# Layer 0, the deformable convolution: a ring of small column tiles in place of two tiles of 18 taps, thirteen gather buffers, twelve combined tiles

## The chip, the cores and the metric

The kernel runs on one core of a Trainium2 chip. The metric is the time of one execution on the device in microseconds (us), taken as the median of several runs. The engines are called as the profile calls them: PE (TensorE, matrix products and transposes; PEld is its weight load), DVE (VectorE), ACT (ScalarE), POOL (GpSimd), SP (SyncE, which only issues transfers here).

## The reference, cut to what matters

A batch of four images (256 channels, 64 by 64 points) goes through four layers, each of the form x = x + layer(groupnorm(x)): a deformable convolution (layer 0), an attention block (layer 1), a grouped deformable operator (layer 2) and a state-space layer (layer 3). Only layer 0 is changed. Cut down, it is:

```python
offset = conv3x3(xn, offset_w) + offset_b             # 18 numbers per point: dy, dx for each of 9 taps
mask = 2 * sigmoid(conv3x3(xn, mod_w) + mod_b)        # 9 numbers per point
for each point p and each of the 9 taps k:
    py, px = p + tap k + offset[k, p]                 # a place between four pixels
    val[:, k, p] = bilinear(xn, py, px) * mask[k, p]  # 4 pixels x 256 channels, weighted
out[o, p] = sum over c, k of weight[o, c, k] * val[c, k, p]
x = x + out
```

So every point needs, for each of nine taps, four pixels of 256 channels from a place that the data decide: 4 KB per point and tap.

## The kernel before, in words

The four images are done one after the other, and layers 0 to 3 one after the other within an image. Layer 0 works from a table in device memory (`tab`) in which one row of 1024 numbers holds the four neighbouring pixels of a place. For the first image the table is built at the start of layer 0; for images 2 to 4 layer 3 of the image before has built it already, with the mean and the deviation (`known`) and the first sixteen sets of points.

The points of an image are 32 tiles of 128 points. A step q is one tap of one tile: 32 x 9 = 288 steps per image. Two tiles go together as a group m, so a group has 18 steps; `where(q)` gives the group, the tile and the tap. Each step passes through these functions, called with a growing lag behind the step number (0, 2, 3, 4, 6, 7):

- `along` (lag 0): POOL issues an indirect transfer (L486) that fetches 128 rows of `tab` into a gather buffer `g` (128 x 1024 numbers, 4 KB per partition, from the pool `pg`). ACT multiplies the left pixels by their weight into a row tile `r` (L496), and DVE adds the weighted right pixels (L497). After L497 the gather buffer is free.
- `across` (lag 2): ACT (L506) and DVE (L507) combine the upper and the lower row into the combined tile `acc` (128 x 256).
- `turn` (lag 3, every second step): PE transposes the two `acc` tiles of one tap into PSUM (L516).
- `copy` (lag 4, every second step): ACT (even taps) or DVE (odd taps) copies the turned columns into `cols` (L523).
- `products` (lag 6): PE multiplies them by the weights `l0w` and sums over the 18 steps of the group in PSUM (L534).
- `add` (lag 7): at a group's end DVE adds the sum to x (L546).

The order on PE, ACT and DVE is written out by hand (`manual_schedule`), so each of them does these steps in the order in which they are called. POOL and SP are not in that list; what they issue is ordered by the scheduler. A buffer's number of copies (`bufs`) says how many steps later its memory may be written again.

In images 2 to 4 more lies beside this at the start. POOL issues the load of the offset weights (`l`, L138). DVE clears the borders of the normalised image `xnp` (L455) and fills 49 rows of it with 14 instructions (L458), ahead of its first L497. PE does the remaining offset convolutions (`offsets`, L372) between the steps, listed in `after`; a part of them follows each of the first 18 steps and every third step after that. They read `xnp` and `l`.

Of the kernel before, what the change touches and what calls it, by code (L numbers as in the profile page):

```python
# [9 lines left out]
F32 = mybir.dt.float32  # L10
# [6 lines left out]
P = 128  # L17
# [46 lines left out]
class Net:  # L64
# [270 lines left out]
    def layer0(self, x, weights):  # L335


        nc, tc = self.nc, self.tc
        tab, known, self.known = self.tab, self.known, None
        with (  # L340
# [2 lines left out]
            tc.tile_pool(name="l0d", bufs=2) as pd,  # L343
            tc.tile_pool(name="l0x", bufs=1) as px,
            tc.tile_pool(name="l0r", bufs=5) as pr,
            tc.tile_pool(name="l0g", bufs=9) as pg,
            ExitStack() as start,
        ):
            self.psum = start.enter_context(self.banks(8))
# [84 lines left out]
            with (  # L434
# [7 lines left out]
                rows, accs, cols, turned, sums = {}, {}, {}, {}, {}  # L442
# [34 lines left out]
                def where(q):  # L477

                    m, r = q // (2 * K2), q % (2 * K2)
                    return m, 2 * m + r % 2, r // 2  # L480
# [18 lines left out]
                def across(q):  # L499

                    _, t, k = where(q)
                    a = accs[q] = pd.tile([P, 256], F32, tag="acc", name="acc", bufs=6)
                    r = rows.pop(q)
                    wy = spots[t // 8][2]
                    t = t % 8
                    nc.scalar.mul(a, r[:, 0, :], wy[:, 0, t, k : k + 1])  # L506
                    nc.vector.scalar_tensor_tensor(a, r[:, 1, :], wy[:, 1, t, k : k + 1], a, ALU.mult, ALU.add)  # L507
# [10 lines left out]
                def copy(q):  # L518
                    if q % 2:
                        m, _, k = where(q)  # L520
                        if k == 0:
                            cols[m] = pd.tile([P, 18, 256], F32, tag="cols", name="cols")
                        (nc.vector.tensor_copy if k % 2 else nc.scalar.copy)(  # L523
                            cols[m][:, 2 * k : 2 * k + 2, :].rearrange("p i c -> p (i c)"), turned.pop(q)
                        )

                def products(q):

                    m, t, k = where(q)
                    i = 2 * k + t % 2  # L530
                    if i == 0:
                        sums[m] = psum2.tile([P, 2, 512], F32, tag="pz", name="pz")
                    for ot in range(2):
                        nc.tensor.matmul(  # L534
                            sums[m][:, ot, :256],
                            wf[:, i, bass.ts(ot, P)],
                            cols[m][:, i, :],
                            start=(i == 0),
                            stop=(i == 17),
                        )  # L540
# [10 lines left out]
                for q in range(steps + 8):  # L551
                    for lag, do in ((0, along), (2, across), (3, turn), (4, copy), (6, products), (7, add)):
                        if 0 <= q - lag < steps:
                            do(q - lag)
                    for do in after.get(q, ()):
                        do()
# [1526 lines left out]
```

## Time and profile before

| | |
|---|---|
| median of 3 runs | 8875.99 us (8872.48 to 8886.61) |
| the profiled execution: its time, its span | 8856.17 us, 8854.4 us |
| busy share of the span: PE, DVE, POOL, ACT | 91%, 88%, 78%, 56% |
| granted PE clock, mean | 0.971 of full speed |
| gather stage, image 1: first L486 to the end of the last L546 | 96.1 to 570.3, 474.2 us |
| image 2 | 2271.7 to 2764.7, 493.0 us |
| image 3 | 4465.3 to 4950.6, 485.3 us |
| image 4 | 6649.5 to 7137.3, 487.8 us |

The four gather stages together take 1940.3 us, 22% of the span. The profile's lines name the source line, the engine, the operation, the tile written and the tile read. An arrow in brackets names what ended the idle time ahead of an instruction; "issue" is idle time without a visible cause, and "remote" is the profile's name for another core or a queue that it does not know.

### The profile page before, as it was taken

The page shows a single profiled execution, that of the slowest core. Times are in us where ns is not written, and L with a number is a line of the kernel's source. Part 1 is how long each engine was busy: PE and PEld are TensorE (multiplying, and loading weights), DVE is VectorE, ACT ScalarE, POOL GpSimd, SP SyncE. Part 2 cuts the span into 40 slices and gives each one's busy share as a digit, 9 for nine tenths or more (in the row PEclk, how much of TensorE's full clock was granted, in tenths as well). Part 3 has the DMA queues.
Part 4 walks back from the last instruction along what each step waited for, and adds up shares of the span by engine and source line. Part 5 has one row for each costly group of instructions (what it writes and reads, how often), then busy time and mean ns, then how long its engine had stood idle before and what let it go on. Part 6 is the DMA issues. An engine that isn't in the chain of part 4 may idle for free.

```text
span 8854.4 us, 96956 instructions
## 1 busy us (share of the span) xinstructions
PE 8048.8 (91%) x31063; PEld 4243.5 (48%) x31063; DVE 7769.1 (88%) x9912; ACT 5001.6 (56%) x7642; POOL 6905.6 (78%) x4407
## 2 busy tenths in 40 slices
PE   6789998998878999899888899989988799989997
PEld 4653474443564347344356435634435643564443
DVE  6788798999888879899988788899998788889998
ACT  4753436666674343666667434376666743446664
POOL 4757797999674779799967477889996747789997
PEclk8999999999999999999999999999999999999999
DMA  8950112445884012244588301123458810122343
GB/s 301 330 180 10 36 57 62 111 114 148 296 321 146 10 41 62 66 113 114 160 308 320 111 10 46 60 81 111 111 171 321 317 68 1 48 63 78 107 107 80
DMA packets 457946, 1149.71 MB, mean 130 GB/s; under 512 B 51425, under 2 KB 119018, under 8 KB 446160
## 3 DMA queue, kind: packets, MB, share of 16 engines
q0 software_dynamic: 178800, 681.04, 23.2%
q1 hardware_dynamic: 278624, 462.37, 16.9%
q8 instruction: 248, 4.06, 0.2%
q14 instruction: 274, 2.24, 0.1%
HBM read 905.84 MB, written 88.10 MB: 112 GB/s over the span
## 4 chain that ended last, share of the span: by engine, by line
DVE 36%; PE 31%; POOL 9%; issue 9%; ACT 6%; DMA 5%; SPq 2%; another core or an unknown queue 1%; DVEq 0%; POOLq 0%; ACTq 0%
DVE h L1906 19%; PE cx L712 11%; DVE h L1815 7%; DMA g<-tab,idx 4%; PE sc L682 3%; POOL h L1930 3%; PE pm L592 3%; DVE r L497 2%; PE pz L534 2%; PE pacc L1036 2%; SPq L889 2%; DVE acc L507 2%; POOL g L486 2%; PE y L1774 2%; ACT r L496 2%
## 5 line engine op out<-in xcount | busy, mean ns | idle before, releaser
L1930 POOL TENSOR_TENSOR h<-h,cn 128x2048 f32<-128x2048 f32 x508 | 2300.5, 4528 | 41.5 <-POOL carry L1927 0.2
L1906 DVE TENSOR_TENSOR_SCAN h<-da,carry,h 128x512 f32<-128x512 f32 x1636 | 1984.6, 1266 | 73.2 <-ACT da L1904 25.1
L1904 ACT ACTIVATE da<-delta,l3a 128x512 f32<-128x512 f32 x2048 | 1392.1, 689 | 1040.5 <-DVE h L1906 1036.3
L1774 PE MATMUL y<-h,ident 128*128 128x512 f32 x4096 | 1908.3, 599 | 4.0 <-POOL h L1930 4.0
L486 POOL DMA_INDIRECT g<-tab,idx x1152 | 1320.2, 1146 | 565.3 <-DVE r L497 269.4
L706 POOL TENSOR_TENSOR acc<-acc,e 128x1024 f32<-128x1024 f32 x472 | 1110.0, 2352 | 353.0 <-ACT e L697 333.9
L534 PE MATMUL pz<-cols,l0w 128*128 128x256 f32 x4608 | 1211.5, 407 | 136.3 <-issue 64.4
L1774 PEld LDWEIGHTS y<-h,ident 128*128 128x128 f32 x4096 | 783.0, 193 | 1017.9 <-issue 950.7
L497 DVE SCALAR_TENSOR_TENSOR r<-g,wx,r 128x512 f32<-128x512 f32 x1152 | 860.3, 747 | 329.4 <-ACT r L496 220.2
L697 ACT ACTIVATE e<-e 128x1024 f32<-128x1024 f32 x512 | 541.3, 1057 | 899.7 <-DVE e L696 793.1
L534 PEld LDWEIGHTS pz<-cols,l0w 128*128 128x128 f32 x4608 | 882.1, 203 | 325.3 <-issue 115.8
L712 PE MATMUL cx<-e,v 128*128 128x512 f32 x2048 | 1002.2, 615 | 2.3 <-ACT e L697 2.3
L496 ACT ACTIVATE r<-g,wx 128x512 f32<-128x512 f32 x1152 | 825.7, 717 | 210.8 <-DMA g<-tab,idx 169.7
L1815 DVE TENSOR_TENSOR h<-du,bn 128x1536 f32<-128x1536 f32 (+1 forms) x512 | 938.5, 1833 | 4.6 <-PE bn L1800 4.4
L1011 DVE TENSOR_TENSOR prod<-ring,A 128x768 f32<-128x768 f32 (+1 forms) x640 | 715.9, 1161 | 48.8 <-DMA ring<-ring 31.5
L696 DVE TENSOR_TENSOR e<-sc,mr 128x512 f32<-128x512 f32 x1024 | 639.1, 682 | 126.0 <-PE sc L682 125.0
L1036 PE MATMUL pacc<-ident,prod 128*128 128x128 f32 x5120 | 664.7, 280 | 47.7 <-POOL prod L1025 18.8
L605 DVE TENSOR_REDUCE m<-pm 128x1 f32<-128x512 f32 x896 | 556.0, 683 | 110.3 <-PE pm L592 110.3
L712 PEld LDWEIGHTS cx<-e,v 128*128 128x128 f32 x2048 | 350.2, 189 | 603.5 <-issue 437.0
L516 PE MATMUL pt<-ident,acc 128*128 128x128 f32 x2304 | 422.4, 292 | 228.1 <-DVE acc L507 179.3
L1036 PEld LDWEIGHTS pacc<-ident,prod 128*128 128x128 f32 x5120 | 564.2, 142 | 136.6 <-POOL prod L1025 50.1
L506 ACT ACTIVATE acc<-r,wy 128x256 f32<-128x256 f32 x1152 | 571.8, 497 | 29.1 <-DVE r L497 24.5
(309 smaller groups left out, 11958.1 us busy)
## 6 DMA issues: line engine op xcount, KB each, us to landing
cn<-cd SPq DMA_DIRECT2D x512, 256.0 KB
bs<-cd SPq DMA_DIRECT2D x412, 256.0 KB
delta<-du POOLq DMA_DIRECT2D x48, 1024.0 KB
tab<-vtnext SPq DMA_DIRECT2D x192, 256.0 KB
ring<-ring SPq DMA_DIRECT2D x288, 126.0 KB
ring<-ring SPq DMA_DIRECT2D x288, 120.0 KB
delta<-w POOLq DMA_DIRECT2D x24, 1024.0 KB
g<-tab,idx POOLq DMA_INDIRECT x1152
```

Of the source, the lines that this page charges most:

```text
L486: nc.gpsimd.indirect_dma_start(out=g[:], out_offset=None, in_=tab[:, :], in_offset=bass.IndirectOffsetOnAxis(ap=spots[t // 8][0][:, t % 8, ...
L496: nc.scalar.mul(r, g[:, :, 0, :], wx[:, 0, t, k : k + 1])
L497: nc.vector.scalar_tensor_tensor(r, g[:, :, 1, :], wx[:, 1, t, k : k + 1], r, ALU.mult, ALU.add)
L534: nc.tensor.matmul(sums[m][:, ot, :256], wf[:, i, bass.ts(ot, P)], cols[m][:, i, :], start=(i == 0), stop=(i == 17),)
L706: nc.gpsimd.tensor_add(b["acc"], b["acc"], e)
L712: nc.tensor.matmul(blocks[qb]["cx"], v[:, 4 * (i + kt // 4 * 4) + kt % 4, :], e[:, bass.ts(i % 2, 512)], start=(kt == 0 and i == 0), stop= ...
L1036: nc.tensor.matmul(d["pd"][:, ct, t, :], prod[:, x, t, bass.ts(ct, P)], self.ident, is_transpose=True, start=(wy == 0 and x == left[0] and ...
L1774: nc.tensor.matmul(c["ys", dc], self.ident, h[:, dc, :], start=False, stop=(n == DS - 1), skip_group_check=(j == 0))
L1815: nc.vector.tensor_mul(h[:, :d, :], c["du"][:, :d, :], c.pop(("bn", n)).to_broadcast([P, d, C]))
L1904: nc.scalar.activation(da, c["delta"][:, dc, :], AF.Exp, scale=al[:, dc, n : n + 1])
L1906: nc.vector.tensor_tensor_scan(h[:, dc, :], da, hb, carry[:, dc, n : n + 1], ALU.mult, ALU.add)
L1930: nc.gpsimd.tensor_mul(h, h, cn.to_broadcast([P, 4, C]))
```

## The change

`cols` was one tile per group, [128, 18, 256], in two copies: 36,864 bytes per partition. It becomes one tile per tap and pair of point tiles, [128, 2, 256], in six copies: 12,288 bytes. The gather buffers go from nine to thirteen (36,864 to 53,248 bytes), and the combined tiles from six to twelve (6,144 to 12,288 bytes). Layer 0's pools are 2,048 bytes smaller in sum, and several of them lie at other addresses than before. The instructions of PE, ACT and DVE in layer 0 are the same in kind and number.

```diff
-            tc.tile_pool(name="l0g", bufs=9) as pg,
+            tc.tile_pool(name="l0g", bufs=13) as pg,
...
-                    a = accs[q] = pd.tile([P, 256], F32, tag="acc", name="acc", bufs=6)
+                    a = accs[q] = pd.tile([P, 256], F32, tag="acc", name="acc", bufs=12)
...
                     if q % 2:
                         m, _, k = where(q)
-                        if k == 0:
-                            cols[m] = pd.tile([P, 18, 256], F32, tag="cols", name="cols")
+                        c = cols[m, k] = pd.tile([P, 2, 256], F32, tag="cols", name="cols", bufs=6)
                         (nc.vector.tensor_copy if k % 2 else nc.scalar.copy)(
-                            cols[m][:, 2 * k : 2 * k + 2, :].rearrange("p i c -> p (i c)"), turned.pop(q)
+                            c.rearrange("p i c -> p (i c)"), turned.pop(q)
                         )
...
                             wf[:, i, bass.ts(ot, P)],
-                            cols[m][:, i, :],
+                            cols[m, k][:, t % 2, :],
```

## The prediction

> **What bounds the kernel now.** The page first, for the lines of the changed stage:
>
> ```profile
> L486 POOL DMA_INDIRECT g<-tab,idx x1152 | 1320.2, 1146 | 565.3 <-DVE r L497 269.4
> L534 PE MATMUL pz<-cols,l0w 128*128 128x256 f32 x4608 | 1211.5, 407 | 136.3 <-issue 64.4
> L497 DVE SCALAR_TENSOR_TENSOR r<-g,wx,r 128x512 f32<-128x512 f32 x1152 | 860.3, 747 | 329.4 <-ACT r L496 220.2
> L496 ACT ACTIVATE r<-g,wx 128x512 f32<-128x512 f32 x1152 | 825.7, 717 | 210.8 <-DMA g<-tab,idx 169.7
> ```
>
> Everybody waits for everybody: POOL for a free buffer (DVE's L497), ACT for a gather that has not landed, DVE for ACT. So I cut the span into windows: the four gather stages, then a stretch of image 2 with offset convolutions, then two short stretches of image 1.
>
> ```profile
> 96.10:570.30 474.20, 376.01 (x1728) 297.99 (x1728) 378.77 (x691) 345.76 (x656) 339.67 (x288) 0.90 0.89 321
> 2271.70:2764.70 493.00, 408.38 (x2041) 300.50 (x2039) 387.58 (x741) 349.59 (x673) 326.53 (x288) 0.93 0.88 317
> 2305.00:2400.00 95.00, 91.80 (x557) 58.61 (x555) 76.84 (x150) 70.43 (x139) 59.66 (x57) 1.00 0.88 313
> 270.00:285.00 15.00, 14.88 (x79) 12.34 (x78) 14.96 (x29) 14.27 (x29) 12.87 (x8) 1.00 0.77 258
> 355.00:361.00 6.00, 5.44 (x28) 4.16 (x27) 5.42 (x11) 5.69 (x11) 4.78 (x5) 1.00 1.02 407
> ```
>
> The columns are window and length, then busy us of PE, PEld, DVE, ACT, POOL, then clock, DMA share, GB/s. No engine is full over a stage: image 1 has PE 376, DVE 379, POOL 340 of 474 us; the transfers run at 321 GB/s though 407 is seen in 355 to 361. In 2305 to 2400 PE is full (91.8 of 95 us): there the gathers do not set the pace. Elsewhere the stage swings. In 270 to 285 DVE is full and POOL issues only 8 gathers in 15 us; at other times DVE starves. The timeline shows why POOL is slow there:
>
> ```profile
> 280.07 4.33 POOL L486 DMA_INDIRECT g<-tab,idx  x1 [0.30 <-DVE r L497]
> 280.32 0.75 DVE L497 SCALAR_TENSOR_TENSOR r<-g,wx,r 128x512 f32<-128x512 f32 x1
> ...
> 283.11 0.48 DVE L507 SCALAR_TENSOR_TENSOR acc<-r,wy,acc 128x256 f32<-128x256 f32 x1
> 283.50 0.68 DVE L546 TENSOR_TENSOR x<-pz,x 128x512 f32<-128x512 f32 x1
> ```
>
> A gather whose median is 0.94 us takes 4.33 us while L497 and L507 follow each other without a gap, and ends just after L546, which reads PSUM. The other half of the swing:
>
> ```profile
> 306.08 0.93 POOL L486 DMA_INDIRECT g<-tab,idx  x1 [0.31 <-issue]
> 308.09 0.58 ACT L523 COPY cols<-pt 128x512 f32<-128x512 f32 x1 [6.57 <-remote]
> 310.35 0.94 POOL L486 DMA_INDIRECT g<-tab,idx  x1 [3.33 <-DVE r L497]
> ```
>
> ACT stands still for 6.57 us at a copy, for a reason that the profile does not name; POOL goes on until the nine buffers are full and then idles 3.33 us. Image 1 has eight such stops of 3.5 to 6.6 us on ACT or DVE.
>
> **The change, part by part.** The *column ring* saves no instruction. The copy of a tap follows the products of the tap twelve steps before on PE, and before that copy ACT or DVE has waited for a later transpose on PE anyway; in the built program the copies wait for PE alone, as before. Price 0, with no cover needed. *Twelve combined tiles* take PE from the semaphores that L507 waits for in the steady state. The line's own view shows no idle time ahead of L507, since `copy` has already tied DVE to PE. Price 0.
>
> *Thirteen gather buffers* are the change. POOL's timeline gives the gap ahead of each gather; 0.30 us is the usual one. What exceeds it and ends in L497 sums to 28.1, 57.8, 44.4 and 49.2 us in images 1 to 4, 179.5 us in all, longest 4.8 us. Four more buffers hold 4 x (0.94 + 0.30) = 4.96 us of issuing, so they cover even the longest of these waits. In images 2 to 4 I leave out the first 130 us, where PE sets the pace: 37.8 + 31.4 + 27.9, with image 1's 27.9 after its first 25 us, makes 125.0 us, or 125.0 / 1.24 = 101 gathers that are issued earlier.
>
> What is one of them worth? In a full stretch such as 270 to 285 POOL delivers 8/15 = 0.533 gathers per us, and DVE takes 1/1.315 = 0.760 steps per us (378.8 us of DVE work over 288 steps). A spare gather then lengthens the stretch by 1/(0.760 - 0.533) = 4.4 us, in which 3.3 steps go at 1.315 us, not at the stage's mean of 1.64: 1.1 us gained. So 101 gathers are worth at most 111 us. The other side agrees: after each stage's first 25 us ACT waits for gathers at L496 for 39.2, 24.6, 25.3 and 27.7 us, 116.8 us together.
>
> I take half of 111, 56 us. What is late next stands close behind: in the same stages ACT's copy waits for PE's transposes (21.5, 44.7, 21.2, 25.4 us), PE is busy 405 to 408 of 485 to 493 us in images 2 to 4, and the unnamed stops stay. The bounds for this term are 0 (a spare gather is eaten up by a slower POOL) and 111. The built program sets a second limit: each gather waits for the landing of the gather eight before it, so thirteen buffers never mean more than eight transfers in flight. POOL's waits for a landing are 26.1 us in 49 waits now; they may grow, at most by what the buffer waits lose.
>
> The rule that speaks against the change is in the Trainium skill, SBUF — State Buffer, section "SBUF: two separate sides": DVE and GpSimd share a port pair as an exclusive lock, and a DVE instruction with two SBUF inputs blocks a GpSimd one that reads SBUF. The 4.33 us gather above fits it (L497 and L507 read two SBUF tiles, a gather its indices); if the rule held without any gap, every us of DVE work gained would block POOL as long, and the sum would be 0, not 56.
>
> *The moved addresses.* At the start of images 2 to 4 the built program differs. Five gathers now stand ahead of the load of `l` on POOL; that load, and DVE's first L455, wait for the last L1606 matmul of layer 3 (before, neither did). The trace of image 2:
>
> ```profile
> 2270.81 0.60 POOL L138 DMA_DIRECT2D l<-in_l  x1 [7.87 <-DVE sres L1875]
> 2271.71 1.04 POOL L486 DMA_INDIRECT g<-tab,idx  x1 [0.30 <-issue]
> 2273.73 6.04 DVE L458 TENSOR_SCALAR xnp<-x,gm,rs 128x64 f32<-128x64 f32 x14
> 2275.02 3.60 PE L1606 MATMUL out<-sres,l3b 128*128 128x512 f32 x8
> 2286.70 0.75 DVE L497 SCALAR_TENSOR_TENSOR r<-g,wx,r 128x512 f32<-128x512 f32 x1 [2.71 <-ACT r L496]
> 2291.29 0.75 DVE L497 SCALAR_TENSOR_TENSOR r<-g,wx,r 128x512 f32<-128x512 f32 x1 [3.44 <-ACT r L496]
> ```
>
> L1606 ends at 2278.6. Gathers 1 to 5 go out 0.9 us earlier, `l` 7.9 us later, and POOL stands some 2 us at it with the sixth gather and all later ones behind. L455 starts at 2278.6 in place of 2272.7, 5.9 us later, and all of ACT's and PE's steps wait behind DVE's first L497 (2279.7, then about 2285.5). Cover: before, DVE's fourth and fifth L497 waited 2.71 and 3.44 us for gathers, so with five gathers landed it has caught up by about 2291. PE's first L372 waits for `l` and `xnp`, some 5 us later, and PE idles 9.2 us between 2281 and 2295 now, waiting for DVE's L507. I price this at +1 us per image, +3 in all; with no cover 3 x 5.9 = +18; if the earlier gathers win, -3.
>
> Sum: 56 - 3 = 53 us. The profiled execution's 8856.2 becomes 8803; it lies 19.8 us below the median of the runs, so the median goes from 8876.0 to **8823**.
>
> **The rivals.** *All starvation goes*: the 111 us term in full, 8876 - 111 + 3 = 8768. For it: the buffers cover every wait, and DVE's 379 us plus the 40 us of image 1's eight stops leave the 474 us stage 55 us of room. Against: PE's waits come next. Chance 0.15.
>
> *No change*: the backlog is eaten up. Thirteen buffers keep DVE gapless longer, POOL stays at 15/8 = 1.88 us per gather, and the stage only swings more slowly; 8876 within 18 us. For it: the 8 gathers in 15 us. Against: during a stop (303.6 to 306.1) POOL issues every 1.24 us and then idles only for want of buffers. Chance 0.22.
>
> *Slower*: the later normalisation is not covered. Place: DVE's queue ahead of the first L497 in images 2 to 4. Price 5.9 us each, and when the late `l` pushes PE's offset convolutions into the PE-bound stretch, up to 8 us each: 3 x 8 = 24, so 8900. It decides if gathers 1 to 5 have landed well before 2285 and PE has no idle time left before the full stretch; and only if the buffers bring nothing. Chance 0.15.
>
> That the rings do nothing is part of the forecast, not a rival.
>
> **How the numbers follow.** The forecast (8823; own range 8785 to 8858, a gain of 18 to 91 us) has 0.48. A change below 0.2%, 18 us, is not told from none here. Faster is 0.48 + 0.15 = 0.63, the same 0.22, slower 0.15. The range 8748 to 8892 reaches past the first rival and most of the way to the last, and leaves out about 0.05 below and 0.13 above.
>
> **What would show it.** POOL's waits for L497 in the gather stages fall from 269 us to below 160 (0.30 each is the floor), ACT's waits for gathers at L496 from 170 to 100 to 130, the stages to 455 to 475 us; L507 and the copies wait as before. Gathers above 1.5 us (22 in image 1, 15 in each other) become more, not fewer: if their excess grows by as much as the waits fall, the second rival is right. In images 2 to 4 DVE's first L497 comes 6 us later after the first gather. The forecast is wrong if the stages keep their length though POOL waits less, or if the unnamed stops grow.

## The result, and the profile after

The change makes the kernel slower: 8932.08 us (median of 6 runs, 8916.75 to 8945.43) against 8881.30 us for the kernel before beside it (8863.04 to 8897.61). The ratio is 1.0052, with a 95% interval of 1.0038 to 1.0065. The forecast was 8823 us with a range of 8748 to 8892: the direction was wrong, and the range did not hold it.

The later sets of runs, each with the kernel before beside it, fall into two conditions: the kernel before takes either about 8890 us (called A here, and so it was for the prediction and the result) or about 8715 us (B), the whole set long and whatever the kernel, and one chip gave both. Every ratio below is taken within one set.

The profiled execution of after has a span of 8915.0 us, 60.6 us more than before's 8854.4. The four gather stages take 500.1, 491.1, 492.8 and 511.1 us, together 1995.1 against 1940.3: 54.8 of the 60.6 us lie there. From line 522 on, line numbers are one lower than before.

The page of after, for the same groups as before (busy us and mean ns of one | idle time before them, and what ended most of it):

```profile
L486 POOL DMA_INDIRECT g<-tab,idx x1152 | 1387.5, 1204 | 560.7 <-issue 232.5
L533 PE MATMUL pz<-cols,l0w 128*128 128x256 f32 x4608 | 1204.3, 406 | 165.2 <-issue 77.7
L497 DVE SCALAR_TENSOR_TENSOR r<-g,wx,r 128x512 f32<-128x512 f32 x1152 | 859.6, 747 | 286.3 <-ACT r L496 140.9
...
L496 ACT ACTIVATE r<-g,wx 128x512 f32<-128x512 f32 x1152 | 825.8, 717 | 165.3 <-DMA g<-tab,idx 140.2
```

POOL's waits for a buffer are no longer the largest cause of its idle time, and ACT waits less for gathers: 140.2 us against 169.7. That is the direction that was forecast, and yet the stages are longer. POOL's mean gather went from 1146 to 1204 ns. The windows of the stages of images 1, 2 and 4 (length, busy us of PE, PEld, DVE, ACT, POOL, clock, DMA share, GB/s):

```profile
96.90:597.00 500.10, 376.83 (x1728) 298.10 (x1728) 377.17 (x692) 342.98 (x656) 362.50 (x288) 0.89 0.85 305
2301.00:2792.00 491.00, 402.71 (x2042) 297.43 (x2040) 387.71 (x742) 347.59 (x673) 344.37 (x289) 0.93 0.89 318
6683.40:7194.40 511.00, 408.40 (x2042) 298.73 (x2040) 387.69 (x742) 349.16 (x673) 338.99 (x289) 0.93 0.85 305
```

PE, DVE and ACT do the same work as before in more time, and the transfers run slower over the stage (305 GB/s in image 1 against 321). The time went into standstills. The list of waits names who waits for whom (sum, count, longest). First before, then after:

```profile
ACT cols L523 <- remote: 135.1, 30, 7.6
...
DVE cols L523 <- remote: 20.1, 9, 4.3
```

```profile
POOL g L486 <- DVE r L497: 232.3, 266, 6.0
...
ACT cols L522 <- remote: 146.0, 28, 13.5
...
DVE cols L522 <- remote: 69.9, 16, 10.8
...
DVE x L545 <- remote: 39.7, 6, 8.2
```

POOL's waits for L497 fell by 37 us only (from 269.4). The stops that the profile puts down to "remote" became longer: 13.5 us at most in place of 7.6. Two of them, one on DVE and one on ACT, in the timeline of after (start, duration, engine, line):

```profile
6933.92 0.72 PE L516 MATMUL pt<-ident,acc 128*128 128x128 f32 x4
...
6934.47 1.89 PE L533 MATMUL pz<-cols,l0w 128*128 128x256 f32 x8
...
6936.20 0.82 PE L516 MATMUL pt<-ident,acc 128*128 128x128 f32 x4
...
6937.83 0.94 POOL L486 DMA_INDIRECT g<-tab,idx  x1 [0.30 <-issue]
...
6944.10 0.95 POOL L486 DMA_INDIRECT g<-tab,idx  x1 [0.30 <-issue]
6944.66 0.69 DVE L522 COPY cols<-pt 128x512 f32<-128x512 f32 x1 [8.13 <-remote]
...
6945.41 3.73 PE L533 MATMUL pz<-cols,l0w 128*128 128x256 f32 x8 [8.38 <-issue]
...
6948.97 0.60 PE L516 MATMUL pt<-ident,acc 128*128 128x128 f32 x4
...
6951.78 0.59 ACT L522 COPY cols<-pt 128x512 f32<-128x512 f32 x1 [13.49 <-remote]
```

The n-th copy of an image needs the n-th four transposes. Those that DVE's copy at 6944.66 needs are the four at 6933.92, which end at 6934.64 by the modelled end. The trace also records updates of the semaphore by which PE tells that it is done: the one for these transposes comes at 6944.64, 10.0 us after the modelled end and 0.02 us before the copy. So "remote" is PE, told late. ACT's copy at 6951.78 needs the four transposes at 6936.20, which end at 6937.03; their update comes at 6951.76. By then PE has run the eight products at 6945.41 and the four transposes at 6948.97, which stand behind them in its order. So what is late is the signal, not PE's work. ACT's semaphore in the same stretch is on time (6938.31, for an L506 that ends at 6938.30). Until 6944.66 POOL issues a gather every 1.25 us; DVE and ACT stand, since their order is fixed and the copy stands ahead of their next blends.

This holds in general. Of the 576 copies in after's gather stages 44 wait longer than 3 us, 265.7 us together, and in 42 of these the copy starts within 0.1 us of an update of PE's semaphore; the transposes that these copies need had ended, by their modelled ends, a median 6.1 and at most 14.8 us earlier. Before has 35 such waits with 168.7 us and a longest of 7.6.

### The profile page after: what moved, and what is told of

The parts are those of the page before. It is cut to its first block, busy times and chain, and to the rows that moved or that the text cites. A ratio compares the mean times of both kernels' runs of the same rounds, so it can differ in the third digit from the quotient of the medians.

```text
span 8915.0 us, 96880 instructions
## 1 busy us (share of the span) xinstructions
PE 8056.2 (90%) x31063; PEld 4247.0 (48%) x31063; DVE 7765.8 (87%) x9912; ACT 4995.7 (56%) x7642; POOL 6976.1 (78%) x4407
## 4 chain that ended last, share of the span: by engine, by line
DVE 37%; PE 29%; POOL 10%; issue 10%; DMA 6%; ACT 5%; SPq 2%; another core or an unknown queue 1%; DVEq 0%; POOLq 0%; ACTq 0%
DVE h L1905 19%; PE cx L711 10%; DVE h L1814 7%; DMA g<-tab,idx 5%; PE sc L681 3%; POOL h L1929 3%; PE pm L591 3%; DVE r L497 3%; POOL g L486 3%; PE pacc L1035 2%; SPq L888 2%; DVE acc L507 2%; PE y L1773 2%; ACT r L496 1%; DVE prod L1010 1%
## 5 line engine op out<-in xcount | busy, mean ns | idle before, releaser
L486 POOL DMA_INDIRECT g<-tab,idx x1152 | 1387.5, 1204 | 560.7 <-issue 232.5
L497 DVE SCALAR_TENSOR_TENSOR r<-g,wx,r 128x512 f32<-128x512 f32 x1152 | 859.6, 747 | 286.3 <-ACT r L496 140.9
L496 ACT ACTIVATE r<-g,wx 128x512 f32<-128x512 f32 x1152 | 825.8, 717 | 165.3 <-DMA g<-tab,idx 140.2
L506 ACT ACTIVATE acc<-r,wy 128x256 f32<-128x256 f32 x1152 | 573.3, 498 | 80.4 <-DVE r L497 54.3
```

The costliest lines, as they stand in the source:

```text
L486: nc.gpsimd.indirect_dma_start(out=g[:], out_offset=None, in_=tab[:, :], in_offset=bass.IndirectOffsetOnAxis(ap=spots[t // 8][0][:, t % 8, ...
L496: nc.scalar.mul(r, g[:, :, 0, :], wx[:, 0, t, k : k + 1])
L497: nc.vector.scalar_tensor_tensor(r, g[:, :, 1, :], wx[:, 1, t, k : k + 1], r, ALU.mult, ALU.add)
```

## The experiments

### Set one, condition A: how many buffers, and which part

```diff
# e1_nine, e1_eleven, e1_seven: after, with
-            tc.tile_pool(name="l0g", bufs=13) as pg,
+            tc.tile_pool(name="l0g", bufs=9) as pg,      # 11, 7
# e1_acc_six: after, with
-  ... name="acc", bufs=12)
+  ... name="acc", bufs=6)
```

> The changed kernel with the gather buffers put back to nine; the ring of turned columns and the twelve combined tiles stay. Theory A (a stop at the copies and adds lasts as long as GpSimd can go on issuing gathers, so more buffers make longer stops): within 0.2% of the kernel before (8881 us beside it), stages of layer 0 that sum to 1930 to 1950 us instead of 1995, and no idle time above 8 us ahead of a copy or an add. Theory B (the ring of columns or the twelve combined tiles are what costs): as slow as the changed kernel, 40 to 55 us above before, stages near 1995. Theory C (the moved addresses at the starts of images 2 to 4): first blend (L497) 15 us after the first gather in images 2 to 4 as in the changed kernel, and 15 to 25 us above before, if the addresses of this version still collide.

> The changed kernel with eleven gather buffers. Theory A: between the two, 20 to 30 us above the kernel before, longest stops 8 to 11 us (two more gathers of 1.25 us than with nine). Theory B: as slow as with thirteen, 40 to 55 us above before. The port theory (the vector engine without pauses blocks GpSimd) expects the gathers' durations above 0.94 us to sum between 238 (before) and 305 (changed).

> The changed kernel with seven gather buffers. Theory A: stops of at most 5 to 6 us, but GpSimd waits for a buffer more often (over 400 us of waits for L497 instead of 269 before); if the stops were the whole cost, 20 to 40 us faster than before; if the earlier accounting of the buffers' worth (1.1 us a gather) holds, 20 to 60 us slower than before. Theory B: as slow as the changed kernel or slower still.

> The changed kernel with six combined tiles instead of twelve; thirteen gather buffers and the ring stay. Theory A: same as the changed kernel within 0.2%, 40 to 55 us above before. If the twelve tiles were the cost, at most 20 us above before.

Measured against 8885.79 us for the kernel before. Waits and gathers are those of the gather stages in one profile each. The row of the kernel before is the profile that the prediction read, that of after, with its ratio, is from the result, and the second row of the kernel before is a profile from set four:

| kernel | ratio (95%) | copies waiting over 3 us: number, sum, longest | gathers' time above 0.94 us | span of the profile |
|---|---|---|---|---|
| seven buffers | 0.9970 (0.9961 to 0.9979) | 34, 132 us, 5.0 us | 191 us | 8846.9 |
| kernel before (nine) | 1 | 35, 169 us, 7.6 us | 239 us | 8854.4 |
| kernel before (nine), set four | 1 | 53, 242 us, 7.8 us | 258 us | 8901.7 |
| nine | 0.9999 (0.9990 to 1.0009) | 48, 230 us, 7.7 us | 239 us | 8891.7 |
| eleven | 1.0049 (1.0035 to 1.0063) | 45, 268 us, 10.9 us | 273 us | 8915.0 |
| thirteen (after) | 1.0052 (1.0038 to 1.0065) | 44, 266 us, 13.5 us | 305 us | 8915.0 |
| thirteen, six combined tiles | 1.0067 (1.0053 to 1.0081) | 45, 308 us, 13.5 us | 287 us | 8924.7 |

The ring of columns and the twelve combined tiles cost nothing: with nine buffers the changed kernel is level with before, and with six combined tiles it is no faster. The buffers are the cost, and fewer of them than before are a gain. That ends theories B and C: in the version with nine, L497 starts 14.5 to 14.8 us after the first gather in images 2 to 4, against 8.0 before, and costs nothing that can be seen. Two expectations missed: with nine buffers the stages sum to 1973 us in place of 1930 to 1950, in a profile that lies 10.8 us above that version's median, and with seven POOL waits 299 us for L497, not over 400.

The longest wait follows the number of buffers. The lists of waits with seven, with nine and with eleven:

```profile
ACT cols L522 <- remote: 101.6, 38, 5.0
```

```profile
ACT cols L522 <- remote: 159.6, 35, 7.7
```

```profile
ACT cols L522 <- remote: 191.5, 33, 10.9
```

From seven to thirteen it grows by 8.5 us in six buffers, 1.4 us each, close to the 1.25 us that POOL needs per gather. This is what theory A says. The sum of these waits differs much between two profiles of the same kernel (169 and 242 us for the kernel before), so one profile's sum does not measure the buffers; but the spans go with the sums, 78 us of span for 176 us of waits from the first row to the last. The buffers set how long a stop can get: in the longest wait of the versions with seven, nine, eleven and thirteen, POOL issued 3, 5, 7 and 9 gathers between the modelled end of the transposes and the copy, and had then stood idle for 1.2 to 2.6 us. Not every stop lasts until POOL has no free buffer left, as theory A has it in full: DVE's above ends while POOL still issues.

### Sets two and three, condition B: no stops, no effect

Set two (kernel before 8712.38 us) and set three (8715.98 us) ran on two other chips.

```diff
# e2_seven_columns_old: before, with bufs=7 for l0g
# e3_thirteen: after; e3_seven: as e1_seven
# e2_seven_later, e2_thirteen_later, e3_thirteen_later: after with 7 or 13 buffers, and
-  for q in range(steps + 8):
-      for lag, do in (..., (4, copy), (6, products), (7, add)):
+  for q in range(steps + 10):
+      for lag, do in (..., (6, copy), (8, products), (9, add)):
# e2_quarter_bytes, e3_quarter_bytes: after, with
-  out=g[:], ... in_=tab[:, :],
+  out=g[:, :256], ... in_=tab.rearrange("r (s c) -> (r s) c", c=256),
-  g = g.rearrange("p (y x c) -> p y x c", y=2, x=2)
+  g = g[:, None, None, :256].to_broadcast([P, 2, 2, 256])
```

> The kernel before with one edit: seven gather buffers instead of nine, its two big column tiles and six combined tiles kept. Theory A (a stop lasts as long as gathers can still be issued): 20 to 45 us faster than before, as seven buffers did in the changed kernel (0.997), longest wait for PE ahead of a copy near 5 us instead of 7.6. Theory B (ring of columns or more combined tiles give what seven buffers showed): no faster than before.

> The changed kernel itself once more, for a second chip: the chip of the second set of runs gave 8712 us for the kernel before (the first gave 8886), and its traces show no wait named remote ahead of a copy. Where the kernel before takes about 8880 us: ratio 1.004 to 1.007 again. Where it takes about 8710: if the stops are the whole cost of the change, ratio 0.996 to 1.002, stages that sum to 1770 to 1800 us; if the change costs something besides the stops (the later first blend in images 2 to 4, three times 6.9 us, or GpSimd's longer gathers), ratio 1.002 to 1.005.

> The changed kernel with seven gather buffers once more. Where the kernel before takes about 8880 us: 0.996 to 0.998 as before. Where it takes about 8710: 0.999 to 1.002 (seven buffers with the old columns gave 0.9997 there), with the first blend 14.6 us after the first gather in images 2 to 4 against 8.0 with the old columns.

Seven buffers with the old columns: 0.9997 (0.9988 to 1.0006). After itself: 0.9998 (0.9989 to 1.0007). Seven buffers in after: 0.9997 (0.9988 to 1.0006). In B the number of buffers makes no difference that can be seen, and no copy of the 576 waits longer than 3 us in the profiles of after, with thirteen or with seven buffers. The waits of after in B:

```profile
POOL g L486 <- DVE r L497: 183.9, 436, 2.5
ACT r L496 <- DMA g<-tab,idx: 182.0, 250, 19.6
...
ACT cols L522 <- PE pt L516: 99.4, 105, 2.7
```

There is no "remote", and every copy that waits starts 0.04 us after the modelled end of its transposes. After's span is 206 us shorter than in A (8709.0 in place of 8915.0), 202 us of it in the four gather stages. Where the stops are missing, the cost of the change is missing too. But the gain that was forecast is missing here too, where no stop can eat it. The windows of image 1 show where it went, with thirteen and then with seven buffers:

```profile
96.30:528.60 432.30, 357.64 (x1728) 278.68 (x1728) 380.81 (x691) 350.59 (x656) 330.73 (x288) 0.97 0.95 352
```

```profile
96.70:525.40 428.70, 362.36 (x1728) 284.83 (x1728) 380.31 (x691) 350.52 (x656) 315.53 (x288) 0.94 0.95 355
```

With thirteen POOL is busy 15.2 us longer for the same 288 gathers. Gap by gap it waits 1.3 us in the whole stage beyond the usual 0.30 us per gather, against 13.4 us with seven; its gathers' time above 0.94 us is 60.2 us against 44.9. The two add up to 61.5 and 58.3 us: each us of waiting that the buffers saved came back as longer gathers. POOL then runs from end to end, 288 x 1.24 + 61.5 = 419 us plus the last steps. In images 2 to 4 the gathers of a stage, from the first to the last, take 79.0 to 86.3 us beyond 288 x 1.24 in both versions, the load of `l` among them.

> The changed kernel with thirteen buffers, in which each gathered row is 1 KB instead of 4 KB (the blends read that quarter four times, so the rows and the result are others; 1152 gathers, all instructions and all waits stay). If the saturated transfers (400 GB/s and more during a stop) make the stops: no wait above 4 us ahead of a copy, idle time ahead of copies and adds under 150 us, stages of 440 us or less. If GpSimd's issuing itself makes them: the stops stay as long as with thirteen buffers (up to 10 to 13 us) with 100 GB/s moved.

> Thirteen buffers with 1 KB rows instead of 4 KB (other rows, other result; all instructions and waits stay). Where the kernel before takes about 8880 us and stops are seen: if saturated transfers make them, no wait named remote above 4 us ahead of a copy and 60 to 180 us faster than the changed kernel; if GpSimd's issuing makes them, the stops stay and the time is within 20 us of it. Where it takes about 8710: about 1.003, as the one run there (8745).

Quarter rows: one run of 8744.96 us in set two, 1.0025 (1.0015 to 1.0036) in set three. The window of image 1 in set three:

```profile
96.20:545.80 449.60, 364.04 (x1728) 285.23 (x1728) 381.11 (x691) 350.90 (x656) 351.49 (x288) 0.95 0.29 87
```

The transfers fill 29% of their time in place of 95%, and the stage is not shorter. So bytes are not what holds it in B. POOL again has no waits to speak of (1.4 us beyond the usual gaps), and its gathers take 80.8 us above 0.94. On the stops this says nothing, since B has none.

> The changed kernel with seven gather buffers and the copies two steps later (lag 6 instead of 4, products 8, adds 9), so that ACT and DVE reach a copy some 2.6 us later than PE's transposes allow. If the stops are late signals from PE of a length that the buffers set (longest 5.0 us with seven), two steps cover more than half of each: waits for PE ahead of copies fall from 236 us (ACT) to under 120 us, stages sum to 1850 to 1890 us instead of 1931, 40 to 80 us faster than seven buffers alone. If the pause of PE, ACT and DVE is one common standstill, whatever they wait for, the waits only move to other lines and the time stays within 0.2% of seven buffers alone (8853 us).

> The changed kernel with the copies two steps later and thirteen gather buffers as in the change. If the signals are late by a length that the buffers set: the longest waits of 13.5 us shrink to about 11 us and those under 3 us vanish, 50 to 90 us faster than the changed kernel. If it is a common standstill: within 0.2% of the changed kernel (8930 us).

> Thirteen buffers with the copies two steps later. Where the kernel before takes about 8880 us and stops are seen: if the stops are late signals from PE, waits ahead of copies named remote fall from 216 us (ACT and DVE together) to under 120 and the time is 20 to 60 us below the changed kernel; if they are a common standstill, within 0.2% of it. Where it takes about 8710: 1.001 again.

Later copies: 1.0018 (1.0009 to 1.0027) with seven buffers, 1.0012 (1.0003 to 1.0021) with thirteen in both sets. With thirteen, in set three:

```profile
ACT r L496 <- DMA g<-tab,idx: 230.4, 328, 20.2
...
POOL g L486 <- DVE r L497: 118.0, 374, 1.0
...
ACT cols L522 <- PE pt L516: 14.7, 11, 2.5
```

ACT's waits for PE's transposes fall from 99.4 to 14.7 us, and its waits for gathers rise from 182.0 to 230.4. What is taken off one wait goes to the gathers, and their mean goes to 1195 ns from 1143. That fits a stage that goes at POOL's own pace in B. It is not shown: the run that would show it, with the gathers freed from DVE in B, was not made.

### Set four, condition A: the gathers freed from the vector engine

```diff
# e4_fixed_psum: after, with one PSUM bank of zeros as second input of both blends
-  nc.vector.scalar_tensor_tensor(r, g[:, :, 1, :], wx[...], r, ALU.mult, ALU.add)
+  nc.vector.scalar_tensor_tensor(r, g[:, :, 1, :], wx[...], zero, ALU.mult, ALU.add)
-  nc.vector.scalar_tensor_tensor(a, r[:, 1, :], wy[...], a, ALU.mult, ALU.add)
+  nc.vector.scalar_tensor_tensor(a, r[:, 1, :], wy[...], zero[:, 0, :], ALU.mult, ALU.add)
# e4_psum_blend (thirteen buffers), e4_psum_blend_nine: ACT writes its half of r to PSUM
-  nc.scalar.mul(r, g[:, :, 0, :], wx[...])
-  nc.vector.scalar_tensor_tensor(r, g[:, :, 1, :], wx[...], r, ALU.mult, ALU.add)
+  h = psum3.tile([P, 2, 256], F32, tag="ph", name="ph")      # two banks
+  nc.scalar.mul(h, g[:, :, 0, :], wx[...])
+  nc.vector.scalar_tensor_tensor(r, g[:, :, 1, :], wx[...], h, ALU.mult, ALU.add)
# in all three: pz is [P, 2, 256] in one bank, with one start and one stop for both sums
```

> The changed kernel with thirteen buffers, in which both blends of the vector engine (L497, L507) take a constant PSUM bank of zeros as second input instead of what ACT wrote to SBUF: each has one SBUF input and one PSUM input, and the first halves of the sums are left out (result differs); to free a bank the two sums of pz lie in one bank. All instructions, buffers and nearly all waits stay. Port theory (GpSimd's gather is blocked while a vector instruction with two SBUF inputs runs): gathers all near 0.94 us, excess over 0.94 us under 60 us in all instead of 234 to 305, GpSimd no longer wall to wall, stages of 400 to 430 us, 80 to 200 us faster than the kernel before. Rival (the transfers or ACT's chain bound the stage): excess may fall but stages stay within 10 us of 432 to 454 (chip without stops).

> The changed kernel with thirteen buffers, in which ACT writes the first half of the blend across x (L496) to a PSUM bank of two, and the vector engine's L497 reads it there and writes r to SBUF; the sums are complete. L507 keeps its two SBUF inputs. Port theory: the part of L497 (860 of 1410 us of such instructions) goes, gathers' excess falls by about 60%, 30 to 120 us faster than the kernel before. Rival: within 0.2% of it, or slower if reading PSUM makes L497 longer than 0.75 us (each 0.05 us is 58 us) or two banks are too few for ACT to run ahead.

> The same with nine gather buffers. Port theory with GpSimd free: buffers decide even less; on a chip without stops within 0.2% of the version with thirteen; on one with stops 30 to 50 us faster than that.

> The kernel before itself, for a trace on this chip. If the chip has no stops (8710 us): no wait named remote ahead of a copy, L486's waits for a buffer 220 to 240 us in all, gathers' excess near 200 us, stages that sum to 1775 to 1795 us.

The set came out in A: the kernel before at 8898.84 us. A line of its page, then its waits:

```profile
L486 POOL DMA_INDIRECT g<-tab,idx x1152 | 1340.6, 1164 | 571.6 <-DVE r L497 271.0
```

```profile
ACT r L496 <- DMA g<-tab,idx: 156.1, 143, 20.3
...
ACT cols L523 <- remote: 147.9, 40, 7.8
ACT cols L523 <- PE pt L516: 141.2, 118, 7.5
```

The same two of the version with zeros in PSUM:

```profile
L489 POOL DMA_INDIRECT g<-tab,idx x1152 | 1087.0, 944 | 826.6 <-DVE r L500 463.9
```

```profile
ACT cols L525 <- PE pt L519: 221.5, 136, 7.6
...
ACT cols L525 <- remote: 202.0, 64, 6.4
...
ACT r L499 <- DMA g<-tab,idx: 48.2, 18, 20.2
```

The port theory is right about the gathers. With one SBUF input in DVE's blends the 1152 gathers take 0.94 us in the mean and 1.26 us at most, the excess over 0.94 falls from 258 to 5 us, and DVE's L500 takes as long as L497 (744 against 749 ns). ACT has few waits for gathers left. The 80 to 200 us that the theory expected did not come. The time is 1.0002 (0.9992 to 1.0011) of before, and the stages sum to 1985 us against 1975. ACT's waits for gathers fell by 108 us, and its waits for PE ahead of the copies rose by 134, to 424 us. In A the supply of gathers does not set the stage. What took its place is the wait for PE's late signals: 98 copies wait over 3 us, 378 us together, in place of 53 and 242.

With the real blend through PSUM the ratio is 1.0018 (1.0009 to 1.0027) with thirteen buffers and 1.0005 (0.9996 to 1.0014) with nine, so thirteen buffers are no better than nine here either. L507 keeps its two SBUF inputs in these two versions, and still the excess is only 15 and 11 us, where the expectation left some 40% of it.

### Set five: the same chip as set four, condition B

> Thirteen buffers with 1 KB rows instead of 4 KB (other rows, other result; instructions and waits stay), for a chip where the kernel before takes about 8890 us. If the transfers make PE's signals late: no wait named remote above 4 us ahead of a copy, stages of 450 to 460 us as on the chips without stops, 130 to 170 us faster than the kernel before. If something of the chip other than the transfers makes them late: stages of 480 to 500 us, within 0.5% of the kernel before. Where the kernel before takes about 8710: 1.0025 again, and the question stays open.

> Seven buffers with the copies two steps later, for a chip where the kernel before takes about 8890 us. If late signals of PE are all that stops ACT and DVE: two steps cover 2.6 us of each, waits ahead of copies under 120 us in all instead of 295 (seven buffers), 40 to 80 us faster than seven buffers alone, so ratio 0.988 to 0.993. If PE's own pace is what bounds the stage there: the waits stay or move to the adds and to PE, ratio 0.996 to 1.000. Where the kernel before takes about 8710: 1.002 again.

The kernel before took 8715.01 us on the chip that had given 8898.84. Quarter rows gave 1.0039 (1.0025 to 1.0052), later copies with seven buffers 1.0026 (1.0017 to 1.0035), both as in B before. So the stops are no property of a chip. Whether the transfers make PE late in A, and whether later copies help there, was not measured.

## Why the prediction was wrong, point by point

Two steps failed: the worth of the thirteen buffers, in both conditions, and the price of the stops, in A.

- **"The unnamed stops stay."** This step failed in A. The stops were read, counted (eight in image 1) and priced at nothing, although the lines shown had POOL issuing all through a stop until the nine buffers were full. They are waits for PE's signal, the longest of them grows with the number of buffers, and the 46 to 51 us by which after is slower go with them: the loss is there in A and is 0 in B, where no such wait is. The prediction named their growth as what would refute it.
- **"Half of 111, 56 us" for the thirteen buffers.** This step failed in both conditions, and it was mis-sized: in B, where no stop interferes, it measures 0 (0.9998). A spare gather was priced by the starvation that it ends, with the later gathers' durations left as they were. They grew by as much as the waits fell: waits and growth together are 61.5 us with thirteen buffers and 58.3 with seven, in image 1. The rival "no change: the backlog is eaten up" described what B shows. In A the term is 0 for another reason: even gathers for which ACT hardly waits (48 us in place of 156) do not shorten the stages (1985 against 1975 us).
- **The rule weighed against the change.** The Trainium skill, SBUF — State Buffer, section "SBUF: two separate sides", taken without any gap as the prediction did, would have made the sum 0. The set with zeros in PSUM agrees with the mechanism (1164 to 944 ns per gather once DVE has one SBUF input), and B agrees with the sum. The versions in which L507 alone keeps two SBUF inputs (952 and 948 ns) show much less blocking than the expectation had left for it. Taking half as a compromise was the mistake: the 4.33 us gather was among the lines read.
- **"Price 0" for the ring and the combined tiles.** Right: 0.9999 with nine buffers.
- **"The moved addresses, +3."** The shift came as said (first L497 at 14.7 to 14.9 us in images 2 to 4 in place of 8.0). Its cost stays inside the interval of the nine-buffer ratio, 8 us at most. The rival that built on it, "Slower", had the right sign for the wrong reason: image 1, which has no such start, lost 25.9 us between the two profiles.
- **What would show it.** POOL's waits for L497 at 232 us in place of under 160; ACT's waits for gathers at 140 in place of 100 to 130; stages of 491 to 511 in place of 455 to 475. Gathers above 1.5 us did become more: 27, 19, 21 and 18 against 22, 15, 15 and 15.

What stays open is why PE reports late in A. What is shown is when. In after, the transfers run at 369 to 415 GB/s during every such wait of over 5 us; in the fastest twentieth of image 2's stage they reach 414 and more. But in B they run above 395 GB/s more often (32% of 2 us slices of after's image 2, against 19% in A) without one late signal, so full transfers alone are not the cause. In A the trace also holds fewer updates of the semaphore than PE instructions that raise it (555 for 655 in after's stages); in B each has its own (655).

The granted clock does not start the stops: in 37 of the 40 copies of after whose signal came over 1 us late, it was full at the modelled end of their transposes. But it falls during the longer ones. In the stop shown (columns as above):

```profile
6943.00:6948.00 5.00, 2.59 (x6) 2.13 (x7) 2.87 (x5) 0.00 (x0) 4.05 (x4) 0.50 1.02 408
```

The eight products behind DVE's copy then take 3.73 us in place of 1.89, so a long stop goes on costing after it has ended.

The best version of those run is the one with seven gather buffers and the rings, 0.9970 in A and 0.9997 in B: the opposite of the change's direction. The blend through PSUM was not run in B, where the gathers seem to set the pace and it could pay.

## What to carry to other kernels

A stop that the profile cannot name is a term of the sum, not a constant: look at what goes on during it, because more buffers let just that go on for longer. Before a wait for buffers is priced as lost time, ask what the issuing engine pays when it no longer waits; here its instructions grew by what the waits shrank. And repeat a small effect in several sets: this one is 0.5% in one condition and nothing in the other.

## What the runs showed of the hardware

- PE's semaphore can come up to 14.8 us after the modelled end of the transposes that raise it, while PE runs the work behind them, and this throughout a set of runs; in another set on the same chip (four and five) every copy that waited started 0.04 us after that end. The profile then names the waits "remote", "issue" or, where the update comes soon after other transposes, PE; the semaphore updates in the trace tell that it is PE.
- DVE's blends stretch the gathers while both kinds have two SBUF inputs (mean 1164 ns, excess 258 us). With L497 reading PSUM, and L507 (553 us of work) still with two SBUF inputs, the mean gather is 952 ns and the excess 15 us, not the 40% that the expectation left to L507. The reverse, L507 alone freed, was not run.
